# A planned two-layer graph network kernel: the planner's ranks, slack and stage orders take new values at set times

## The chip, the cores and the metric

The kernel runs on one core of a Trainium2 chip. The metric is device time in microseconds (us) of one execution of the whole program; several executions are made and their median is given. A profile is one more execution, with its own time.

In this text PE is the engine that multiplies matrices (with PEld, its weight loads), DVE the vector engine, ACT the engine for activation functions, POOL the general-purpose engine and SP the engine that issues most DMAs (transfers). PSUM is the memory that PE writes to; it has eight banks. Each engine works through its own queue of instructions in order.

## The reference

The input is a batch of 64 graphs with 256 nodes each, 256 features a node, and an integer adjacency matrix a graph. Two layers follow each other; all numbers are 32-bit floats.

```python
def _gat(h, adj, W, a, out_features):
    Wh = jnp.matmul(h, W)
    e = jax.nn.leaky_relu(jnp.matmul(Wh, a[:out_features]) + jnp.swapaxes(jnp.matmul(Wh, a[out_features:]), 1, 2), negative_slope=0.2)
    att = jax.nn.softmax(jnp.where(adj > 0, e, NEG), axis=1)
    return jnp.matmul(att, Wh)

# layer 0
h = _gat(_gat(x, adj, W1, a1, Fout), adj, W2, a2, W2.shape[1])
h = _layernorm(x + h, g_ln1, b_ln1)
x = _layernorm(h + jax.nn.relu(h @ w_ff1 + b_ff1) @ w_ff2 + b_ff2, g_ln2, b_ln2)      # 256 -> 1024 -> 256

# layer 1: 8 heads of 32, four value matrices Wv[r], one for each value of adj
attn = softmax(q @ k.T / sqrt(32))
out = sum over r of (attn * (adj == r)) @ (x @ Wv[r] + bv[r])
x = _ln(x + out @ Wo + bo, g1, beta1)
x = _ln(x + gelu(x @ W1 + b1) @ W2 + b2, g2, beta2)
```

## The kernel before

**Pairs and stages.** The 64 graphs are worked on as 32 pairs. A pair goes through four stages (`whole_way`): `gat_layers` (the two graph attentions of layer 0), `feed_forward` with relu, `attention` (layer 1) and `feed_forward` with gelu. Several pairs are under way at a time, each in another stage. The names "gat", "ff" and "attention" can each be held by one pair at a time.

**The matmuls.** The products of the first feed-forward layer and of q, k and v are made by the class `Blocks`: seven products of half-size blocks (steps p1 to p7, each 0.86 us in the plan) instead of eight, with the sums between them done by DVE (line 449, rank "blocks") and copies out of PSUM by ACT (line 757 in feed-forward, rank "copies"; line 763 applies the activation function, rank "act"). "a1" is product 1 of the first half of the work, "b3" product 3 of the second; `FIRST` and `QKV` are the orders in which these steps are taken, and "s0" and "s1" in `QKV` are the scores of the first two groups of heads. The second feed-forward layer (`by_seven`) has seven products of 64 matmuls, with DVE sums of the inputs (`combine`, line 831, rank "sums") and DVE additions of the results to the rows (line 828, rank "last"). Nearly all matmuls are issued by `by_strips` at line 122, four strips of 32 columns each. The scores (line 943) are multiplied in tiles of another shape, 32 rows. A group of scores takes four PSUM banks; ACT exponentiates them (line 952, rank "exp"), DVE masks them (956, "mask") and adds halves (960, "halves"), and `products` (lines 974 and 977) multiplies them by the values. `GROUPS` is the order of these groups of scores and products. `layernorm` uses ACT for squares (659), DVE to centre (668) and scale (671), and POOL for the root (664, 665); `means` (645, ACT) is the mean after `by_seven`. `transposed` turns rows on DVE (692, rank "turn") and sends them by SP through a scratch buffer back to SBUF as `yT`; attention copies that on ACT (883, rank "piece").

**The planner.** When the program is built, `run` simulates the engines with a clock each, and emits instructions in the order in which the simulation takes them. That order is final: `keep_order` chains each engine's instructions. Work for DVE, ACT, POOL and SP is handed in with `put`, with a duration, the events that it needs and a rank. When an engine is free, it takes of the pieces that are ready the one of the lowest rank (`RANK`), and of equal ranks the one that was ready first. PE is filled by Python generators, one a pair: each yields the events, the names and the banks that its next step needs, and `took` moves PE's clock by the step's duration. A step is sure if it was ready `SLACK` (0.3 us) ago; of the sure ones the one of the lowest `DEGREE` of its kind (first, gat, attention, fill, rows) is taken, and if none is sure the one that is ready first. A change of tile shape costs 0.1 us of plan time. `FLIGHT` (6) is the number of pairs that may be begun. All these are constants for the whole plan.

The chip follows the emitted order, with its real durations; where they differ from the plan's, an engine waits on semaphores.

```python
able = [n for at, n in times if at <= now]
...
sure = [n for at, n in times if at <= now - SLACK]
g = going[min(sure, key=lambda n: (going[n][0] is besides, degree(going[n]), n))
          if sure else min(times)[1]]
...
piece = waiting[engine].pop(min(able, key=lambda n: (waiting[engine][n]["rank"], waiting[engine][n]["first"]["ready"])))
```

Of the kernel before, what the change touches and what calls it, by code (L numbers as in the profile page):

```python
# [18 lines left out]
P = 128  # L19
# [9 lines left out]
SHAPES = ("rows",)  # L29
SLACK = 0.3  # L30
FLIGHT = 6
RANK = {"adj": 1, "second": 0.5, "blocks": -1, "exps": 1.5, "addends": 0.5, "weigh": 3, "ratios": -0.5, "squares": 0.5,
        "copies": -2, "act": -1, "last": -1, "sums": -0.5, "qk": 1, "v": 1.5, "exp": 3, "mask": 0, "halves": 0, "invert": 3,
# [9 lines left out]
def two_layers(ctx: ExitStack, tc: tile.TileContext, t: dict, out: bass.AP, flag: bass.AP):  # L43
# [70 lines left out]
    psum = ctx.enter_context(tc.tile_pool(name="psum", bufs=8, space=bass.MemoryType.PSUM))  # L114

    def bank():
        return psum.tile([P, 512], F32, name="ps")

# [37 lines left out]
    clock = dict(START)  # L156
    waiting = {engine: [] for engine in engines if engine != "tensor"}
    alone, filling, shaped = {}, [], [None]
    free = {name: [0.0] * n for name, n in (("bank", 8), ("a", HQ), ("m", HQ), ("h", HQ), ("yb", 1), ("yT", 2), ("yTa", 1),
# [80 lines left out]
    def run(besides, ways, together):  # L240
# [7 lines left out]
        def degree(g):  # L248
            kind = ("fill" if g[0] in filling else "first" if "ff" in (g[2] or ()) or alone.get("ff") is g[0] else
                    "attention" if "attention" in (g[2] or ()) or alone.get("attention") is g[0] else "gat")  # L250
            return DEGREE["after" if shaped[0] and shape(g) else shape(g) or kind]

        together += 1
        while True:
            while len(going) < together and (way := next(ways, None)) is not None:
                going.append([way, *next(way)])
# [21 lines left out]
            if engine == "tensor":  # L278
                sure = [n for at, n in times if at <= now - SLACK]
# [10 lines left out]
                if step is None:  # L290
                    together -= g[0] is besides
                    going.remove(g)
                else:
                    g[1:] = step
# [23 lines left out]
    def load(pair, at=None):  # L318
# [29 lines left out]
        def in_bytes(there):  # L348
            return put("vector", 1.35, largest, put("scalar", 1.2, small_adj, there, needs="adj", rank=RANK["adj"]), rank=RANK["adj"])
# [51 lines left out]
    class Second:  # L401


        def __init__(self, b, name, *events):
            self.b, self.name, self.there, self.read = b, name, [], []
            for n in range(3):
                self.there.append(put("vector", 0.34, lambda n=n: self.add(n), *events, rank=RANK["second"], needs=None if n else name))
                events = self.there[-1:]
            self.there.append(Event())
# [8 lines left out]
        def read_by_second(self, event):  # L418
            self.read.append(event)
            if len(self.read) == 2:  # L420
                put("vector", 0.34, lambda: self.add(3), self.there[2], *self.read, rank=RANK["second"], event=self.there[3])
# [7 lines left out]
    class Blocks:  # L429
# [5 lines left out]
        def __init__(self, second, first, begin, multiply, target, copy, corner, finished):  # L435
            self.second, self.first, self.begin, self.bank, self.u3, self.fifth = second, first, begin, {}, None, None
            self.multiply, self.target, self.copy, self.corner, self.finished = multiply, target, copy, corner, finished

        def product(self, n, to, a, first=False):
            if first:  # L440
                self.bank[to] = self.bank[to] if n == 5 else bank().rearrange("p (n c) -> p n c", n=2)
# [5 lines left out]
        def add(self, c, h, bank, *events, frees=()):  # L447
            def add():
                nc.vector.tensor_tensor(self.target(c, h), self.bank[bank], self.target(c, h), ALU.add)  # L449
            there = put("vector", 0.6, add, *events, rank=RANK["blocks"], frees=frees)  # L450
            self.finished(c, h, there)
            return there

        def p1(self):
            yield *self.first, 1
            self.begin()
            self.u1 = self.copy(0, 0, self.product(1, "x", 0, True))

        def p2(self):
            yield [], None, 1  # L460
            there = self.product(2, "z", 1, True)
            self.c11 = self.add(0, 0, "z", self.u1, there)
            self.second.read_by_second(there)

        def p5(self):
            yield [self.c11, self.second.there[0]], None, 0
# [3 lines left out]
        def p6(self):  # L470
            yield [self.u1, self.second.there[1]], None, 0
            self.u2 = self.copy(0, 1, self.product(6, "x", 3))

        def p7(self):
            yield [self.u2, self.second.there[2]], None, 0
            self.u3 = self.copy(1, 1, self.product(7, "x", 4))
            self.add_fifth()

        def add_fifth(self):
            if self.u3 and self.fifth:  # L480
                self.c22 = self.add(1, 1, "z", self.u3, self.fifth)

        def p4(self):
            yield [self.u3, self.second.there[3]], None, 0
            self.corner(self.bank["x"], self.product(4, "x", 6))

        def p3(self):
            yield [self.c22], None, 0
            self.add(0, 1, "z", self.u2, self.product(3, "z", 5), frees=["bank"])


    def addends(y, there, at, layer, pair):
# [20 lines left out]
        there = put("scalar", 0.6, exps, *there, rank=RANK["exps"], function="exp")  # L513
# [28 lines left out]
        there = put("vector", 0.2, turn, there, rank=RANK["addends"])  # L542
# [3 lines left out]
    def gat_weights(y, at, at_home, ratio, there, to, b):  # L546
# [20 lines left out]
        there = put("vector", 0.95, lambda: weigh(0), *there, rank=RANK["weigh"] + b / 2, needs="e")  # L567
        there = put("vector", 1.13, lambda: weigh(1), there, rank=RANK["weigh"] + b / 2, frees=["rows"] * b)
        return of, put_each("scalar", 0.4, [lambda j=j: scale(j) for j in range(2)], there, rank=RANK["ratios"])

    def gat_layers(pair, to, loads):
# [3 lines left out]
        def evacuated(to, k, wide, ps):  # L575
            return put("scalar", 0.3, lambda: nc.scalar.activation(to[:, k, :wide], ps[:, :wide], AF.Copy),
                       took(0.88), rank=RANK["evac"], frees=["bank"])
# [30 lines left out]
        for b in range(2):  # L608
# [9 lines left out]
            transposed(to["x"], layernorm(to["x"], ln[0], b, added, biased[0]), normal, b, pair, 0)  # L618
# [4 lines left out]
    def add_rows(y, p, b, *events):  # L623
# [12 lines left out]
        return of, put_each("vector", 0.44, [lambda j=j: add(j) for j in range(2)], *events, rank=RANK["rows"], frees=["bank"])  # L636

    def means(y, b, *events):
# [8 lines left out]
        return of, put_each("scalar", 0.54, [lambda j=j: mean(j) for j in range(2)], *events, rank=RANK["means"])  # L647

    def layernorm(r, gb, b, added, *events):
# [11 lines left out]
        def root():  # L661
# [3 lines left out]
            nc.gpsimd.tensor_tensor(rstd, rstd, mhalf[:, :2], ALU.pow)  # L665

# [6 lines left out]
        there = put_each("scalar", 0.54, [lambda j=j: square(j) for j in range(2)], there, rank=RANK["squares"])  # L673
        centred = put_each("vector", 0.4, [lambda j=j: centre(j) for j in range(2)], there, rank=RANK["centre"])
        there = put("gpsimd", 1.2, root, there, rank=0)
        return put_each("vector", 0.4, [lambda j=j: scale(j) for j in range(2)], there, centred, *events, rank=RANK["scale"])
# [5 lines left out]
    def transposed(y, ready, to, b, pair, stage):  # L682
# [23 lines left out]
        there = put("vector", 0.62, turn, ready, rank=RANK["turn"], needs="yb")  # L706
# [25 lines left out]
    def feed_forward(y, normal, w, func, relieved, gb, pair, stage):  # L732
# [11 lines left out]
        def slabs(t):  # L744
# [11 lines left out]
            def copy(c, h, event):  # L756
                return put("scalar", 0.5, lambda: nc.scalar.activation(target(c, h), blocks.bank["x"], AF.Copy), event, rank=RANK["copies"])  # L757

            def activate(c, h, event, of=None, frees=()):
                for n in range(2):  # L760
# [3 lines left out]
                        to, source, func, bias=b1[:, m:m + 1]), event, rank=RANK["act"] + h, function=kind,  # L764
# [4 lines left out]
            blocks = Blocks(second, first, begin, multiply, target, copy,  # L769
                            lambda of, event: activate(1, 0, event, of, ["bank"]), activate)  # L770
            return blocks
# [3 lines left out]
        for step in FIRST:  # L775
            yield from steps[step]()
        yield from (by_seven if stage in SEVEN else by_eight)(y, normal, f, evacuated, w2, w2_there, b)
        for g in range(2):
            normal[g] = layernorm(y, gb, g, normal["added"][g], *([biased[1]] if onwards else []))
# [5 lines left out]
    def by_eight(y, normal, f, evacuated, w2, w2_there, last):  # L785
# [3 lines left out]
        for g in range(2):  # L789
            for j in range(2):  # L790
                for part in (order[:half], order[half:]):
# [8 lines left out]
                    if g == j == 0 and part[0] == 0:  # L800
                        yield from last.p3()
# [3 lines left out]
    def by_seven(y, normal, f, evacuated, w2, w2_there, last):  # L805
# [14 lines left out]
        def product(n, to, side, first=False):  # L820
# [4 lines left out]
            return took(1.8)  # L825

        def add(to, of, us, *events, frees=()):
            return put("vector", us, lambda: nc.vector.tensor_tensor(to, of, to, ALU.add), *events, rank=RANK["last"], frees=frees)  # L828

        def combine(to, a, b, op, *events):  # L830
            return put("vector", 1.14, lambda: nc.vector.tensor_tensor(to, a, b, op), *events, rank=RANK["sums"])  # L831

        def two_halves():
            return bank().rearrange("p (j b d) -> p j b d", j=2, b=2)
# [6 lines left out]
        yield [w2_there, *done(0, 0)], None, 1  # L841
        left = two_halves()
# [4 lines left out]
        x = two_halves()[:, 0]  # L847
# [3 lines left out]
        yield from last.p3()  # L851
# [3 lines left out]
        v = two_halves()[:, 0]  # L855
# [6 lines left out]
        d24 = add(rows[:, :, :, :P], left, 0.6, read2, read4, frees=["bank"])  # L862
# [9 lines left out]
    def attention(y, normal, pair, all_adj):  # L872
# [13 lines left out]
        there = put("scalar", 0.52, lambda: in_one_piece(0), normal[0], rank=RANK["piece"], needs="yTa")  # L886
        there = put("scalar", 0.52, lambda: in_one_piece(1), there, normal[1], rank=RANK["piece"], frees=["yT"])
# [27 lines left out]
        def with_bias_qk(c, b, event, frees=()):  # L915
# [654 lines left out]
```

## Time and profile before

| what | value |
| --- | --- |
| median of 3 executions | 2944.82 us (2944.0 to 2946.82) |
| the profiled execution: its time | 2945.81 us |
| the profiled execution: its span, first to last instruction | 2944.0 us |
| PE busy / DVE busy / ACT busy | 2881.8 / 2618.9 / 1859.3 us |
| mean granted clock of PE | 0.992 |
| largest group on PE: the 128x128 matmuls of the second feed-forward layers | 14336 of 419.1 us busy and 14336 of 422.5 |
| largest group on DVE: the masks (L956) and the sums (L831) | 256 of 311.2 us busy and 256 of 310.4 |
| largest group on ACT: the exponentials (L952) | 512 of 269.8 us busy, 600 ns each |

The span is the time from the first to the last instruction in the profile; the time of an execution also has what lies around it. Busy time is the union of an engine's instructions. A view of stretches gives for each window its length, then busy time and number of instructions of PE, PEld, DVE, ACT and POOL, then the granted clock of PE (1.00 is full), the share of the DMA engines and GB/s. A line of waits reads: who waited, for what, how many us in all, how many times, the longest. A line of the timeline reads: start, us busy, engine, line, operation, tiles, shape, count and, in brackets, idle time before it and what ended that. "ps" is a PSUM bank, "ff" an intermediate of feed-forward.

### The profile page before, as it was taken

What the parts mean: (1) busy time and instruction counts of PE and PEld (TensorE: products, weight loads), DVE (VectorE), ACT (ScalarE), POOL (GpSimd) and SP (SyncE); (2) the same over time, 40 slices, a digit from 0 to 9 for tenths busy, and PEclk for the clock granted to TensorE, in tenths of its full rate; (3) what the DMA queues carried; (4) which work ended last, traced back from release to release, by engine and by line L of the source; (5) the groups of instructions that cost most, each with busy time, mean ns of one, the idle gap of its engine ahead of it and who ended that gap; (6) DMA issues with size and microseconds to landing.
All of it is one profiled execution on the core that took longest, in us unless ns stands there. A gap on an engine that the chain in (4) does not pass through costs nothing.

```text
span 2944.0 us, 147796 instructions
## 1 busy us (share of the span) xinstructions
PE 2881.8 (98%) x66066; PEld 2025.8 (69%) x66066; DVE 2618.9 (89%) x5873; ACT 1859.3 (63%) x5124; POOL 267.4 (9%) x518
## 2 busy tenths in 40 slices
PE   6999999999999999999999999999999999999998
PEld 4776766667767667767677667677666666676776
DVE  5899999889988889988889989899988898889886
ACT  3666666666665666665766665766665665666555
POOL 0010100010000100000101000100110100011001
PEclk7999999999999999999999999999999999999999
DMA  6222222222122221222221222221222221222100
GB/s 181 69 69 71 75 65 84 67 85 71 60 74 75 89 75 61 70 68 85 88 76 61 69 70 85 83 81 51 69 75 82 82 74 55 72 69 70 44 3 25
DMA packets 214179, 211.84 MB, mean 72 GB/s; under 512 B 22945, under 2 KB 173089, under 8 KB 213537
## 3 DMA queue, kind: packets, MB, share of 16 engines
q1 hardware_dynamic: 213120, 202.06, 21.5%
q8 instruction: 520, 8.52, 1.2%
q14 instruction: 123, 1.00, 0.1%
q10 hardware_dynamic: 416, 0.26, 0.0%
HBM read 137.51 MB, written 64.73 MB: 69 GB/s over the span
## 4 chain that ended last, share of the span: by engine, by line
PE 64%; DVE 27%; issue 3%; ACT 2%; DMA 2%; SPq 1%; POOL 0%; DVEq 0%; POOLq 0%; ACTq 0%
PE ps L122 56%; DVE ff L831 4%; PE ps L974 4%; DVE m L956 3%; PE ps L943 3%; DVE ff L449 3%; DVE x L671 2%; DVE x L668 2%; DVE h L960 2%; DVE x L828 2%; DVE yb L692 2%; PE ps L977 1%; DVE x L631 1%; DVE e L558 1%; DMA home<-yb 1%
## 5 line engine op out<-in xcount | busy, mean ns | idle before, releaser
L952 ACT ACTIVATE a<-ps 128x512 f32<-128x512 f32 x512 | 269.8, 600 | 297.0 <-PE ps L943 274.1
L122 PE MATMUL ps<-w_L_gnn_W,ff 128*32 128x128 f32 x14336 | 419.1, 273 | 16.3 <-DVE ff L831 10.7
L122 PEld LDWEIGHTS ps<-w_L_gnn_W,ff 128*32 128x32 f32 x14336 | 394.5, 110 | 44.1 <-DVE ff L831 18.3
L122 PE MATMUL ps<-w_L_gnn_w_ff,ff 128*32 128x128 f32 x14336 | 422.5, 273 | 1.0 <-DVE ff L449 0.5
L122 PEld LDWEIGHTS ps<-w_L_gnn_w_ff,ff 128*32 128x32 f32 x14336 | 389.6, 110 | 41.2 <-issue 16.6
L122 PE MATMUL ps<-yT,w_L_gnn_W1p 128*32 128x256 f32 x5120 | 313.9, 379 | 1.5 <-DVE qk L997 0.8
L122 PE MATMUL ps<-yT,w_L_gnn_w_ff1p 128*32 128x256 f32 x5120 | 312.8, 379 | 2.2 <-ACT ff L757 2.1
L831 DVE TENSOR_TENSOR ff<-ff 128x1024 f32<-128x1024 f32 x256 | 310.4, 1212 | 4.3 <-PE ps L122 3.6
L449 DVE TENSOR_TENSOR ff<-ps,ff 128x512 f32<-128x512 f32 x384 | 259.0, 679 | 61.3 <-ACT ff L757 42.7
L664 POOL TENSOR_SCALAR rstd<-squares 128x2 f32<-128x2 f32 x256 | 70.6, 276 | 2649.3 <-ACT unread L659 2647.3
L956 DVE TENSOR_TENSOR m<-a,adj 128x1024 f32<-128x1024 f32 x256 | 311.2, 1215 | 0.0
L659 ACT ACTIVATE unread<-x,less 128x256 f32<-128x256 f32 x512 | 259.1, 506 | 80.5 <-DVE less L634 48.6
L757 ACT ACTIVATE ff<-ps 128x512 f32<-128x512 f32 x384 | 225.3, 591 | 102.6 <-PE ps L122 100.6
L763 ACT ACTIVATE ff<-ff,c_L_gnn_b 128x256 f32<-128x256 f32 x384 | 174.7, 503 | 131.6 <-DVE ff L449 131.0
L122 PE MATMUL ps<-xw,e 128*32 128x258 f32 (+1 forms) x4096 | 246.1, 386 | 6.8 <-ACT xw L565 6.8
L122 PEld LDWEIGHTS ps<-yT,w_L_gnn_W1p 128*32 128x32 f32 x5120 | 165.7, 110 | 111.2 <-DVE qk L997 1.8
L122 PEld LDWEIGHTS ps<-yT,w_L_gnn_w_ff1p 128*32 128x32 f32 x5120 | 166.6, 110 | 107.5 <-ACT ff L757 3.6
L763 ACT ACTIVATE ff<-ff,c_L_gnn_b_ff 128x256 f32<-128x256 f32 x384 | 176.7, 502 | 75.9 <-DVE ff L449 75.6
L828 DVE TENSOR_TENSOR x<-ps,x 128x256 f32<-128x256 f32 (+1 forms) x384 | 192.7, 502 | 28.6 <-PE ps L122 26.4
L665 POOL TENSOR_TENSOR rstd<-rstd,mhalf 128x2 f32<-128x2 f32 x256 | 196.1, 766 | 21.3
L122 PEld LDWEIGHTS ps<-xw,e 128*32 128x32 f32 x4096 | 133.1, 112 | 90.7 <-ACT xw L565 9.0
L960 DVE TENSOR_TENSOR h<-a 128x512 f32<-128x512 f32 x256 | 174.7, 682 | 0.0
(132 smaller groups left out, 4969.9 us busy)
## 6 DMA issues: line engine op xcount, KB each, us to landing
home<-yb SPq DMA_DIRECT2D x182, 256.0 KB, 2.1
yT<-home SPq DMA_DIRECT2D x728, 64.0 KB, 2.1
rows<-row SPq DMA_DIRECT2D x60, 512.0 KB, 4.3
input<-in_xT SPq DMA_DIRECT2D x32, 512.0 KB, 4.0
x<-in_x SPq DMA_DIRECT2D x32, 512.0 KB, 3.9
out<-x SPq DMA_DIRECT2D x64, 256.0 KB, 3.3
input<-in_adjT SPq DMA_DIRECT2D x30, 512.0 KB, 4.1
v<-in_adjT SPq DMA_DIRECT2D x2, 512.0 KB, 7.3
```

The source lines that it names most:

```text
L122: nc.tensor.matmul(to[at:at + DH], lhsT=lhsT[:, at:at + DH], rhs=rhs, **flags)
L449: nc.vector.tensor_tensor(self.target(c, h), self.bank[bank], self.target(c, h), ALU.add)
L659: nc.scalar.activation(unread, rows[j], AF.Square, bias=of["less"][:, j:j + 1], accum_out=squares[:, j:j + 1])
L665: nc.gpsimd.tensor_tensor(rstd, rstd, mhalf[:, :2], ALU.pow)
L757: return put("scalar", 0.5, lambda: nc.scalar.activation(target(c, h), blocks.bank["x"], AF.Copy), event, rank=RANK["copies"])
L763: evacuated[h][m] = put("scalar", 0.4, lambda m=m, to=to, source=source: nc.scalar.activation(to, source, func, bias=b1[:, m:m + 1]), even ...
L828: return put("vector", us, lambda: nc.vector.tensor_tensor(to, of, to, ALU.add), *events, rank=RANK["last"], frees=frees)
L831: return put("vector", 1.14, lambda: nc.vector.tensor_tensor(to, a, b, op), *events, rank=RANK["sums"])
L952: nc.scalar.activation(a[n][q][:, k], ps[2 * q + k], AF.Exp)
L956: nc.vector.tensor_tensor(m[n][q], a[n][q], adj, ALU.mult)
L960: nc.vector.tensor_tensor(h[n][q], a[n][q][:, :, :N], a[n][q][:, :, N:], ALU.add)
L974: nc.tensor.matmul(po[o * DH:(o + 1) * DH, :N], lhsT=v[:, b, jc, at:at + DH], rhs=e[o // 2][:, o % 2, jc * N:(jc + 1) * N], start=r == jc ...
```

## The change

A table `CHANGES` gives, for times of PE's clock in the plan 90 us apart, new values of ranks, of degrees and of the settings "slack", "flight", "first", "qkv" and "groups". `run` puts them in force once PE's planned clock has passed their time. A stage that is under way keeps the order that it began with.

```diff
+NORMED = ()
+CHANGES = (
+    (27.0, ("all", "slack", 0.2), ("rank", "means", 0)),
+    (117.0, ("rank", "means", 1)),
+    (207.0, ("all", "qkv", ("a1", "b1", "b2", "a2", "a6", "a5", "b6", "a7", "a4", "b5", "b7", "a3", "b4", "s0", "b3", "s1")),
+     ("rank", "adj", 1), ("rank", "normalise", 2), ("rank", "exp", -1)),
+    (297.0, ("degree", "fill", 1), ("all", "groups", (([0], []), ([1], []), ([], [2]), ([], [3]), ([2], []), ([3], []))),
+     ("degree", "first", -1), ("all", "slack", 0.3)),
+    (387.0, ("degree", "fill", 2.5), ("all", "slack", 0.8), ("rank", "mask", 1.5), ("rank", "turn", 2),
+     ("all", "first", ("a1", "b1", "a6", "a2", "b2", "b6", "a5", "a7", "b7", "a4", "b5", "b4", "a3"))),
+    (477.0, ("all", "slack", 0.1)),
+    (657.0, ("rank", "qk", 2), ("rank", "adj", 0), ("rank", "act", 0.5), ("rank", "last", 0.5)),
+    (1197.0, ("rank", "invert", 1.5), ("rank", "adj", -1), ("rank", "exps", -0.5),
+     ("all", "first", ("a1", "b1", "a2", "a6", "b2", "b6", "a5", "a7", "b7", "a4", "b5", "b4", "a3")),
+     ("rank", "normalise", 0), ("degree", "rows", 2)),
+    (1287.0, ("rank", "turn", 1)),
+    (1377.0, ("all", "groups", (([0], []), ([1], []), ([], [2]), ([], [3]), ([2], []), ([3], []))), ("rank", "divide", 1.5),
+     ("rank", "copies", -2), ("all", "flight", 5)),
+    (1467.0, ("all", "first", ("a1", "b1", "a2", "a6", "b2", "b6", "a5", "a7", "b7", "b5", "a4", "b4", "a3")),
+     ("rank", "addends", 0.5)),
+    (1557.0, ("rank", "copies", 1), ("rank", "qk", -2)),
+    (1827.0, ("rank", "copies", -2)),
+    (1917.0, ("rank", "v", 1)),
+    (2007.0, ("rank", "rows", 1.5), ("rank", "squares", -0.5), ("rank", "copies", 0)),
+    (2367.0, ("rank", "last", 1), ("rank", "adj", -0.5), ("degree", "attention", 0)),
+    (2547.0, ("rank", "divide", 1), ("rank", "mask", 3)),
+    (2637.0, ("degree", "first", 2.5)),
+    (2727.0, ("rank", "last", 3), ("rank", "second", 0.5)),
+    (2817.0, ("all", "first", ("a1", "b1", "a2", "a6", "b2", "b6", "a5", "a7", "b7", "b5", "a4", "b4", "a3")),
+     ("rank", "second", -0.5), ("rank", "rows", -2)),
+)
+KEPT = 0
+SEEDS = {"ff": (), "qk": (), "v": ()}
...
         while True:
-            while len(going) < together and (way := next(ways, None)) is not None:
+            while changes and clock["tensor"] >= changes[0][0]:
+                _, of, name, value = changes.pop(0)
+                of[name] = value
+            while len(going) < settings["flight"] + any(g[0] is besides for g in going) and (way := next(ways, None)) is not None:
                 going.append([way, *next(way)])
...
-                sure = [n for at, n in times if at <= now - SLACK]
+                sure = [n for at, n in times if at <= now - settings["slack"]]
...
-        there = put("vector", 0.95, lambda: weigh(0), *there, rank=RANK["weigh"] + b / 2, needs="e")
+        there = put("vector", 0.93, lambda: weigh(0), *there, rank=rank_of["weigh"] + b / 2, needs="e")
...
-            return put("scalar", 0.3, lambda: nc.scalar.activation(to[:, k, :wide], ps[:, :wide], AF.Copy),
-                       took(0.88), rank=RANK["evac"], frees=["bank"])
+            return put("scalar", 0.27, lambda: nc.scalar.activation(to[:, k, :wide], ps[:, :wide], AF.Copy),
+                       took(0.88), rank=rank_of["evac"], frees=["bank"])
...
-        return of, put_each("scalar", 0.54, [lambda j=j: mean(j) for j in range(2)], *events, rank=RANK["means"])
+        return of, put_each("scalar", 0.45, [lambda j=j: mean(j) for j in range(2)], *events, rank=rank_of["means"])
...
-            return took(1.8)
+            return took(1.745)
...
-        for step in FIRST:
+        order = settings["first"]
+        for step in order:
             yield from steps[step]()
```

Everywhere else `RANK[...]` becomes `rank_of[...]`, a copy of the table that `CHANGES` writes to. Beside this, the diff restructures `Blocks`, `by_seven` and `layernorm` so that banks can be set aside (`KEPT`), sums can be started in PSUM (`SEEDS`, rank "seeds") and a layernorm can be scaled on ACT (`NORMED`, rank "normalise"). With `KEPT` at 0 and the other two empty, as here, these branches do nothing, but for one new tile `nothing` of 128x1 that DVE sets to zero at the start:

```diff
+    nothing = const.tile([P, 1], F32, name="nothing")
+    nc.vector.memset(nothing, 0.0)
+    kept = [kept_bank() for _ in range(KEPT)]
```

## The prediction, made before the result was known

> **What bounds the kernel now.** First the page's head, for the engine nearest to the span, then the chain that ended last, for what the end hangs on.
>
> ```profile
> span 2944.0 us, 147796 instructions
> PE 2881.8 (98%) x66066; PEld 2025.8 (69%) x66066; DVE 2618.9 (89%) x5873; ACT 1859.3 (63%) x5124; POOL 267.4 (9%) x518
> ...
> PE 64%; DVE 27%; issue 3%; ACT 2%; DMA 2%; SPq 1%; POOL 0%; DVEq 0%; POOLq 0%; ACTq 0%
> ```
>
> PE (the matmuls) leaves 62 us of the span idle. DVE holds 27% of the chain because the chain follows whatever released a step, and DVE is nearly as full; it doesn't mean that PE stood still for it. So I cut the span into stretches of 90 us, about one pair each, and read PE's busy time, the first number after the comma.
>
> ```profile
> 27.00:117.00 90.00, 79.99 (x1460) 55.37 (x1456) 63.86 (x176) 45.71 (x129) 6.88 (x12) 0.83 0.32 91
> ...
> 387.00:477.00 90.00, 87.75 (x2044) 61.45 (x2040) 82.66 (x188) 56.73 (x159) 9.05 (x18) 1.00 0.24 76
> 477.00:567.00 90.00, 87.05 (x1992) 60.91 (x1986) 77.36 (x170) 56.54 (x153) 6.72 (x12) 0.98 0.23 73
> ...
> 657.00:747.00 90.00, 89.73 (x2076) 62.85 (x2072) 82.34 (x185) 58.43 (x163) 8.35 (x17) 1.00 0.23 73
> ...
> 2187.00:2277.00 90.00, 87.95 (x1996) 60.65 (x1992) 81.34 (x177) 59.43 (x163) 8.88 (x16) 1.00 0.23 76
> 2277.00:2367.00 90.00, 87.85 (x2032) 61.13 (x2024) 82.28 (x191) 57.13 (x159) 7.87 (x16) 1.00 0.24 77
> 2367.00:2457.00 90.00, 87.36 (x1992) 60.19 (x1988) 78.83 (x178) 59.55 (x160) 9.10 (x16) 1.00 0.22 69
> ```
>
> The middle (657 to 2007) is periodic: the chain's longest pieces start at 889.55, 978.33, 1067.11, ... us, 88.78 us apart, and PE idles 0.27 us in 90. No plan can take more than that idle there without changing the matmuls, of which this change changes none. The loose time is in four places. Start: 10.0 us idle in 27:117. From 117 on, the 31 stretches idle 28.1 us together (2790.0 less 2841.89 - 79.99 = 2761.9 busy); at the steady rate they would idle 31 x 0.28 = 8.7, so **19.4 us are irregular**, mostly between 207 and 657 and between 2007 and 2637. Third, a stall of 0.20 us that most pairs of the middle repeat, some 17 times, 3.4 us. Fourth, the edges: 6.55 us before the first matmul (a weight's DMA) and 11 us after the last one.
>
> PE's own waits say who is late:
>
> ```profile
> PE ps L122 <- DVE ff L831: 11.1, 26, 2.1
> PE ps L122 <- ACT xw L565: 6.8, 2, 4.4
> ...
> PE ps L122 <- DVE ff L449: 5.0, 5, 1.9
> ...
> PE ps L122 <- ACT ff L757: 3.9, 6, 1.0
> PE ps L122 <- ACT ff L763: 3.6, 2, 2.5
> ```
>
> L831 is `combine`, the sums that the second feed-forward layer needs; L449 adds up a block of the first. Both are DVE work whose place in DVE's queue is set by a rank (`sums`, `blocks`) against all other ranks. L565 belongs to the start.
>
> **The change part by part.** *What is off.* KEPT is 0 and SEEDS and NORMED are empty, so the new branches of `Blocks`, `by_seven` and `layernorm` emit what was emitted before; `normalise` and `seeds` rank nothing. New is one memset of 128x1, at most 0.14 us (L503's row of a 128x1 result), under the 6.55 us that PE waits for its first weight: 0. Both forms of the count of pairs in flight give the same. Flight 5 from 1377 on: `x` has four buffers, and only one pair is in each of `gat`, `ff` and `attention`, so a sixth pair could only wait: 0. The entries of 1377 for `groups` and of 2817 for `first` set the value that stands: 0.
>
> *Durations.* They are the planner's, and move no instruction by themselves. `by_seven`'s product goes from 1.8 to 1.745: PE's timeline has 64 such matmuls at 1291.48 and the next block at 1293.23, so 1.75. The old value put PE 14 x 0.05 = 0.7 us a pair later than it is, so a `combine` looked ready when it wasn't; that fits the 0.20 us that repeats. I take **-1.5** of the 3.4 (bounds 0 and -3.4).
>
> *Ranks and degrees, for the irregular stalls.* Of PE's waits, those on DVE (11.1 and 5.0 above, and 1.7 on L828 and 0.8 on L997 further down the same list: 18.6, less the repeated 3.4) are 15.2 us, and those are a matter of order: DVE is idle 7.6 us of 90 in the steady stretch, and ranks of `mask`, `turn`, `rows`, `last` moved back let sums go first. Ranks on ACT matter less: `exp` goes from last to near the front at 207, but before its instructions (L952) ACT idles 297 us in all, 274 of them waiting for PE's scores, so they go at once already. Stalls by way of ACT are less in reach. The longest, 2.52 us before 538.41, has ACT holding at a copy of `yT` for its DMA (1.92 us idle) with the activation PE needs behind it; the lags that the planner gives to DMAs stay as they are. I take two thirds of 15.2: **-10** (bounds 0, and all 19.4). A matmul that isn't late then meets the next limit, DVE's queue at 82 of 90, so not all can go.
>
> *The clock.* After that stall the granted clock is half for 3.4 us (0.98 in that stretch), which costs 1.7. Gone with it, or elsewhere again: **-1** (0 to -1.7). The Trainium skill (TensorE: Matmul & The Clock Gate, "Why this matters for your kernels") says that the clock holds if no gap is over about 3 us. Here 2.52 us were enough, while 2.05 us before 2232.43 were not. By the rule this term would be 0.
>
> *Stage orders.* `first`, `qkv` and `groups` permute the same matmuls. What they can save is a change of tile shape: the scores (32 rows) stand alone at every place of the timeline that I read.
>
> ```profile
> 1282.76 1.26 PE L122 MATMUL ps<-yT,w_L_gnn_w_ff1p 128*32 128x256 f32 x20
> 1283.95 1.15 PE L943 MATMUL ps<-qk 32*128 32x256 f32 x16
> 1285.03 3.70 PE L122 MATMUL ps<-w_L_gnn_w_ff,ff 128*32 128x128 f32 x128
> ```
>
> From 1283.95 to 1285.03 are 1.08 us for 16 matmuls that elsewhere take 0.86, and 0.11 lie ahead of them: 0.33 us for each lone group, four a pair. The new `groups` puts the third and fourth next to each other. But each needs four of eight banks, which ACT frees at 0.60 us an exponential, and other steps hold some: an actual meeting is rare. **-1** (bounds 0, and two meetings a pair in 29 pairs, 19). Moving b3 between s0 and s1 only fills the wait for banks: 0.
>
> *Slack.* From 477 to the end a step counts as sure when it was ready 0.1 us ago by the plan, not 0.3. What is queued behind a wrong guess is all of PE, in order. The trace's error of one step isn't shown, but the repeated 0.20 us is what one wrong guess costs. I take 0.13 us a pair over 27.4 pairs: **+3.5** (bounds 0, and four such stalls a pair, 0.8 x 27.4 = 22).
>
> *Start and end.* At 27 only `means` and the slack move; the 4.62 us before the weights for v and the 3.0 before the first transposes wait for loads and for a first chain that nothing overlaps: 0 (4 either way). At the end only DVE's order changes, under PE: 0.
>
> **Sum:** -1.5 - 10 - 1 - 1 + 3.5 = -10. The profiled execution took 2945.81 (2944.0 span, 1.8 around it), 1.0 over the median 2944.82; the median less 10 is **2935 us**.
>
> **Rivals.**
> (1) *All stalls go.* Every irregular and repeated stall and the clock's loss: -24.5, 2920; with half of the scores meeting, 2911. For it: the periodic middle shows that PE can run with 0.27 idle. Against: yT's DMAs, and 32 pairs with one rank table each need luck at the joints.
> (2) *Reshuffled.* The stalls come at other places with the same sum: 2945, 5 either way. For it: the plan after 27 us is a new one everywhere, the middle's included, which has nothing to gain. Against: the stalls come in two clusters, which looks like orders that didn't suit them.
> (3) *Too little slack: slower.* From 477 on PE goes ahead of sums and activations that are 0.1 to 0.3 us late. Four stalls of 0.2 a pair cost 22, less the 13.5 otherwise won: 2953 or more. It decides, past 0.2%, from (13.5 + 5.9) / 27.4 = 0.7 us a pair, that is when PE idles 1.0 in 90 in the middle. For it: the steady period already has such a stall in most pairs. Against: the durations are nearer to the rows now, and a wait under 0.2 is often absorbed.
>
> **How the numbers follow.** Forecast (2927 to 2938.9) 0.50; all go (below 2927) 0.14; reshuffled 0.19; slower 0.17. About 0.2%, 5.9 us, is what a measurement of this kernel tells from no change. Faster by more: 0.50 + 0.14 = 0.64; within: 0.19; slower: 0.17. From the rivals' ends I leave out the part under 2918 (0.06) and over 2953 (0.12): range **2918 to 2953**; the forecast alone 2927 to 2939.
>
> **What would show it.** PE idle from 117 on falls from 28 to about 18 us: right; the two clusters gone but the middle over 0.6 idle in 90: the slack's term was too small. The wait on L831 down from 11.1 to under 6 confirms ranks and durations. Fewer than 128 separate L943 groups: the scores meet. The granted clock at 1.00 in all stretches after 117: the clock's term. Wrong altogether if the middle's period leaves 88.8 us by over 0.3 either way, which is 4 us or more by itself, or if the stretch 27:117 moves by over 4.

## The result, and the profile after

The changed kernel takes **2929.66 us** (median of 6, 2921.04 to 2935.39) against 2946.19 for the kernel before (median of 6, 2944.0 to 2950.51): ratio **0.9938**, 95% interval 0.992 to 0.9956. That is faster, by 16.5 us between the medians. The profiled execution took 2928.64 us, with a span of 2926.9, 17.1 shorter than before's 2944.0.

First the page's head and the chain of the changed kernel.

```profile
span 2926.9 us, 147784 instructions
PE 2874.6 (98%) x66066; PEld 2062.1 (70%) x66066; DVE 2629.6 (90%) x5874; ACT 1847.4 (63%) x5120; POOL 274.1 (9%) x518
...
PE 4%; DVE 2%; ACT 1%; issue 0%; DMA 0%; POOL 0%; DVEq 0%; SPq 0%; POOLq 0%; ACTq 0%
```

The number of matmuls is the same. Of the 17.1 us, PE's idle time gives 9.9 (62.2 to 52.3) and its busy time 7.2. As the matmuls are the same, that is the clock (some 5 us, half of the 10 us by which its times at half clock are shorter) and the small joints between blocks. The chain is of no use here: its shares add up to 7%, because it could be followed back only to a DMA at 2693 us. So the stretches must carry the reading. In each line the first number after the comma is PE's busy time.

```profile
27.00:117.00 90.00, 85.64 (x1644) 57.99 (x1640) 71.42 (x198) 53.70 (x148) 6.66 (x12) 0.91 0.38 110
...
387.00:477.00 90.00, 89.98 (x1956) 60.66 (x1948) 83.03 (x190) 61.51 (x171) 8.10 (x16) 1.00 0.24 73
477.00:567.00 90.00, 90.00 (x2164) 64.92 (x2164) 81.26 (x194) 61.03 (x166) 11.34 (x20) 1.00 0.27 84
...
837.00:927.00 90.00, 86.77 (x1988) 59.81 (x1980) 78.59 (x177) 56.96 (x155) 8.41 (x16) 0.98 0.23 70
927.00:1017.00 90.00, 87.55 (x2020) 61.01 (x2016) 80.49 (x182) 57.05 (x159) 8.70 (x16) 1.00 0.23 69
...
1197.00:1287.00 90.00, 87.23 (x1980) 60.42 (x1976) 76.83 (x179) 54.90 (x155) 8.80 (x16) 0.98 0.25 78
...
2187.00:2277.00 90.00, 90.00 (x2086) 63.78 (x2082) 83.91 (x191) 58.47 (x166) 7.92 (x16) 1.00 0.24 73
2277.00:2367.00 90.00, 89.95 (x2069) 69.96 (x2064) 82.57 (x185) 57.92 (x162) 7.72 (x16) 1.00 0.23 73
2367.00:2457.00 90.00, 90.00 (x2076) 79.04 (x2072) 82.17 (x181) 60.86 (x168) 10.57 (x20) 1.00 0.23 73
```

Three things are to be seen. The start idles 4.4 us instead of 10.0. Both clusters of stalls are gone: PE idles 0.8 us between 207 and 657 (8.2 before) and 0.2 us between 2007 and 2637 (11.5 before). And the middle, which had been nearly clean, is not: between 657 and 2007 it idles 15.3 us (6.4 before), most of it from 837 to 1287. Two of the same stretches in the kernel before, the first of them one of the two in its middle that idle over 1 us:

```profile
837.00:927.00 90.00, 88.53 (x2052) 61.91 (x2046) 81.05 (x183) 57.38 (x160) 8.06 (x17) 1.00 0.24 73
...
1197.00:1287.00 90.00, 89.72 (x2100) 63.35 (x2096) 82.28 (x188) 58.47 (x163) 7.82 (x16) 1.00 0.23 73
```

Since both kernels do the same matmuls, I weigh each matmul of the trace by its columns, add them up, and compare the times at which the two have done the same amount of work. A negative number: the changed kernel is ahead.

| stretch (time in the kernel before) | changed in it, us | ahead at its end, us |
| --- | --- | --- |
| 0 to 71 | -10.0 | -10.0 |
| 71 to 205 | +3.4 | -6.6 |
| 205 to 679 | -11.2 | -17.8 |
| 679 to 886 | -1.9 | -19.7 |
| 886 to 1402 | +12.6 | -7.1 |
| 1402 to 2020 | +1.0 | -6.1 |
| 2020 to 2649 | -13.6 | -19.7 |
| 2649 to 2918 | +2.7 | -17.0 |

PE's waits name the engines:

```profile
PE ps L166 <- ACT xw L650: 10.6, 5, 3.2
...
PE ps L166 <- ACT xw L639: 5.8, 2, 5.4
...
PE ps L166 <- ACT ff L845: 2.2, 3, 1.4
...
PE ps L166 <- DVE ff L920: 1.3, 3, 0.6
```

L920 is `combine` (L831 before): its 11.1 us are down to 1.3. L650 is `evacuated`, ACT's copy of the graph attention's products out of PSUM (L576 before); no wait of PE on it stood in the list of before, and it is the largest now. The half-clock time at the start is 24 us (20.1 to 30.4, 40.6 to 47.5, 54.3 to 61.1) against 37.5 before; half of the difference, 6.7, is most of what the start gains beside 3.7 less idle.

Why L650 is late stands in the timeline around the longest such stall:

```profile
882.13 0.63 ACT L973 ACTIVATE yTa<-yT 128x512 f32<-128x512 f32 x1 [2.93 <-DMA yT<-home]
882.66 0.40 ACT L719 ACTIVATE unread<-x 128x256 f32<-128x256 f32 x1
...
886.63 0.51 ACT L733 ACTIVATE unread<-x,less 128x256 f32<-128x256 f32 x1
...
887.14 0.64 ACT L650 ACTIVATE xw<-ps 128x258 f32<-128x258 f32 x2
...
887.56 3.38 PE L166 MATMUL ps<-yT,w_L_gnn_w_ff1p 128*32 128x256 f32 x32 [3.23 <-ACT xw L650]
```

ACT stands 2.93 us at the copy of `yT` into `yTa`, which waits for its DMA; eight activations stand between that and the two copies that free PE's banks, and PE has idled 3.23 us. SP's own waits show that the DMAs are in a new situation: before a gather of `yT`, SP waited for the store's landing 93.4 us in 55 waits before, and 313.9 us in 136 waits now. The line of the kernel before comes first.

```profile
SPq L703 <- DMA home<-yb: 93.4, 55, 4.3
```

```profile
SPq L791 <- DMA home<-yb: 313.9, 136, 5.5
```

### The profile page after: what moved, and what is told of

It reads as the page before. It is cut to its first block, busy times and chain, and to the rows that moved or that the text cites. A ratio compares the mean times of both kernels' runs of the same rounds, so it can differ in the third digit from the quotient of the medians.

```text
span 2926.9 us, 147784 instructions
## 1 busy us (share of the span) xinstructions
PE 2874.6 (98%) x66066; PEld 2062.1 (70%) x66066; DVE 2629.6 (90%) x5874; ACT 1847.4 (63%) x5120; POOL 274.1 (9%) x518
## 5 line engine op out<-in xcount | busy, mean ns | idle before, releaser
L166 PEld LDWEIGHTS ps<-w_L_gnn_w_ff,ff 128*32 128x32 f32 x14336 | 397.3, 110 | 36.3 <-issue 13.0
L166 PE MATMUL ps<-yT,w_L_gnn_w_ff1p 128*32 128x256 f32 x5120 | 321.4, 382 | 10.8 <-ACT xw L650 10.6
L920 DVE TENSOR_TENSOR ff<-ff 128x1024 f32<-128x1024 f32 x256 | 311.2, 1215 | 16.0 <-PE ps L166 12.6
L738 POOL TENSOR_SCALAR rstd<-squares 128x2 f32<-128x2 f32 x256 | 78.2, 306 | 2625.1 <-ACT unread L733 2622.5
L166 PEld LDWEIGHTS ps<-yT,w_L_gnn_w_ff1p 128*32 128x32 f32 x5120 | 172.6, 110 | 113.6 <-ACT xw L650 13.5
L166 PEld LDWEIGHTS ps<-yT,w_L_gnn_W1p 128*32 128x32 f32 x5120 | 171.9, 110 | 100.1 <-ACT ff L845 5.7
L917 DVE TENSOR_TENSOR x<-ps,x 128x256 f32<-128x256 f32 (+1 forms) x384 | 191.8, 504 | 33.8 <-PE ps L166 30.4
L1007 ACT ACTIVATE qk<-ps,bqk 128x256 f32<-128x256 f32 x256 | 109.3, 468 | 118.3 <-PE ps L166 117.3
```

Source lines behind the costliest of these rows:

```text
L166: nc.tensor.matmul(to[at:at + DH], lhsT=lhsT[:, at:at + DH], rhs=rhs, **flags)
L738: nc.gpsimd.tensor_scalar(rstd, squares, 1.0 / D, EPS, ALU.mult, ALU.add)
L1007: nc.scalar.activation(target_qk(c, b)[:, n], of[:, n], AF.Identity, bias=bqk[:, n, c:c + 1])
```

## The experiments

The planner has a clock of its own, so each plan states how long PE idles in it. That gives a theory with numbers. **Theory A**: the chip follows the plan; what the table does is take idle time out of the plan, as one piece fitted to the four durations. The main rival, **B**: small differences between plan and chip swamp this, and the new time is a draw among plans of the same kind. After the profile came **theory F** for the new stalls: ACT held by the DMA, with PE's copies queued behind.

### Parts of the change alone

Four kernels: the durations alone, the table with the old durations, the table's first two entries, and its entries up to 477.

```diff
-CHANGES = (
-    (27.0, ...
+CHANGES = ()
```

> The changed kernel with an empty table: the four new durations alone. Theory A (the chip follows the planned order, and PE idles about where the plan has it idle): the plan's PE clock has 140 us of idle here, against 57 in the kernel before and 19 in the changed one, so the time is about 2946 + 83 = 3029 us, between 3000 and 3050. Rival B (small differences between plan and chip swamp the plan's idle; any plan of this kind gives about the same): 2946, 15 either way. Rival C (better durations are a gain by themselves, as the prediction's term of -1.5 has it): 2935 to 2945.

```diff
-        there = put("vector", 0.93, lambda: weigh(0), ...
+        there = put("vector", 0.95, lambda: weigh(0), ...
...
-            return took(1.745)
+            return took(1.8)
```

> The changed kernel with its table but the old four durations. Theory A: the plan idles 103 us, 46 more than before, so about 2992 us, between 2975 and 3015. Rival B: 2946, 15 either way. Rival D (the table's orders are good whatever the durations are): 2925 to 2940, near the changed kernel.

```diff
     (117.0, ("rank", "means", 1)),
-    (207.0, ("all", "qkv", ...
...
+)
```

> New durations and only the table's entries at 27 and 117. Up to 297 the planned orders are those of the changed kernel. Theory A: the start up to 60 us on the chip keeps the gain of 10 us that the changed kernel has there, and after that the plan idles 3.07 us in every 90, so PE idles about 2 to 4 us in each stretch of the middle; the plan has 101 us of idle, so about 2946 + 43 = 2989 us, 2970 to 3010. Rival B: 2946, 15 either way.

```diff
     (477.0, ("all", "slack", 0.1)),
-    (657.0, ("rank", "qk", 2), ...
...
+)
```

> New durations and the table's entries up to 477, held from there on. Up to 657 the planned orders are those of the changed kernel. Theory A: the gain up to 657 stays (16 to 18 us ahead of the kernel before); after that the plan idles 1.0 us in 90, about the 0.93 of the kernel before, and 18 us near 2850 which it doesn't have; the plan's idle is 66 us, 9 over that of before, so about 2955 us, 2940 to 2975. Rival E (the entries after 657 do nothing, since the plan of before is periodic there and has nothing to gain): 2925 to 2935, like the changed kernel.

Then two that leave out one kind of entry: all for the slack, and all for stage orders. The second of them leaves out more than its expectation says: with the order "first" went the two entries for the degree of the kind "first", at 297 and at 2637.

```diff
-    (27.0, ("all", "slack", 0.2), ("rank", "means", 0)),
+    (27.0, ("rank", "means", 0)),
...
-    (477.0, ("all", "slack", 0.1)),
```

> The changed kernel without the table's entries for slack: 0.3 all along. Theory A, now with a scale: in the six kernels measured so far the time is the plan's last PE time, at the new duration of a product, plus 33 to 74 us, 57 on average. Here the plan ends PE at 2979, so 3036 us, between 3012 and 3053. Rival I (the slack's term of the prediction: less slack costs 3.5 us, so 0.3 all along is a little better than the table): 2922 to 2932.

```diff
-    (207.0, ("all", "qkv", ...), ("rank", "adj", 1), ...
+    (207.0, ("rank", "adj", 1), ...
...
-     ("degree", "first", -1), ("all", "slack", 0.3)),
+     ("all", "slack", 0.3)),
...
-    (2637.0, ("degree", "first", 2.5)),
```

> The changed kernel without the table's entries for stage orders (first, qkv, groups): the orders of before all along, with the table's ranks, degrees and slack. Theory A: the plan ends PE at 2991, so 3048 us, between 3024 and 3065. Rival J (the orders' term of the prediction: they are worth 1 us): 2927 to 2934.

In the table the plan's last PE time is given at 1.745 us a product; for the two plans with 1.8 that takes 448 x 0.055 = 24.6 us off, time that the chip doesn't take, since a product there lasts 1.75 us.

| kernel | PE idle in the plan | plan's last PE time | measured median | ratio to before (95%) |
| --- | --- | --- | --- | --- |
| before | 57 | 2900 | 2946.19 | |
| changed | 19 | 2862 | 2929.66 | 0.9938 (0.992 to 0.9956) |
| durations alone | 140 | 2983 | 3016.16 | 1.0243 (1.0226 to 1.0261) |
| table, old durations | 103 | 2946 | 3019.24 | 1.0258 (1.0238 to 1.0278) |
| entries at 27 and 117 | 101 | 2944 | 3001.22 | 1.0189 (1.0171 to 1.0207) |
| entries up to 477 | 66 | 2909 | 2971.22 | 1.0089 (1.0067 to 1.0112) |
| without slack | 136 | 2979 | 3052.19 | 1.0364 (1.034 to 1.0388) |
| without stage orders and the degree of "first" | 148 | 2991 | 3043.16 | 1.0329 (1.0312 to 1.0346) |

**Each of the six kernels with only some of the change is slower than the kernel before**, by 0.9 to 3.6%, and all six are as slow as theory A has it, to within 27 us (the one with the old durations is 4 us above A's range). B, C, D, E and I fall. J isn't tested: the kernel without stage orders lacks the two degrees as well, so no run says what the orders are worth by themselves. The time is the plan's last PE time plus 33 to 74 us. So the plan is a good guide for large differences, and a poor one for the last 20 us: of the 38 us that the change takes out of the plan (57 to 19), 17 arrived.

Where the plan idles says the same. In the plan of the kernel before, PE idles 10 us between 207 and 657 and 13 us between 2007 and 2637, in that of the changed kernel 3 and 0: the two clusters stood in the old plan, and the new one has taken them out. But from 657 to 2007 the plan goes from 14 us of idle to 0.04, and the chip from 6.4 to 15.3. That is where the gain of the plan didn't arrive.

The durations alone show how a part can be a loss. A stretch of their middle, and PE's waits:

```profile
1557.00:1647.00 90.00, 87.87 (x2030) 61.46 (x2024) 79.56 (x182) 57.29 (x159) 8.01 (x16) 1.00 0.21 70
```

```profile
PE ps L137 <- ACT a L1017: 28.6, 21, 1.4
PE ps L137 <- DVE ff L891: 23.8, 34, 1.4
PE ps L137 <- ACT xw L621: 16.2, 21, 0.8
```

The plan settles in another period there, with 4.2 us idle in 90 in the plan and 2 to 3 on the chip (2.1 in the stretch shown, 2.9 in most). New durations shorten nothing by themselves; they only make the planner take other orders, and the single rank table that had suited the old durations doesn't suit the new ones. (Nor are all four nearer to the trace: two accumulating copies of L645, planned at 0.54 before and 0.45 now, follow each other by 0.54 us from start to start in the trace of before.) The entries up to 477 give the other half of the picture. On the chip that kernel is 14 us ahead of the kernel before when that has come to 575 us (the changed kernel: 17), and then loses all of it: it is level at 1917, and ends 25 us behind, as the plan loses 18 us in the stretch from 2817. Against rival E: the later entries gain nothing over the kernel before until 2020 us, but without them the gain of the first 600 us doesn't last.

### Who holds ACT

The emission of one instruction can be changed while the plan stays as it is. Here the copy of `yT` goes to POOL; PE, DVE, SP and the rest of ACT keep their order.

```diff
-            nc.scalar.activation(yT[:, b].rearrange(...), normal["yT"][:, b].rearrange(...), AF.Copy)
+            nc.gpsimd.tensor_copy(yT[:, b].rearrange(...), normal["yT"][:, b].rearrange(...))
```

> The changed kernel with one thing moved: the copy of yT into yTa, which waits for a DMA, is done by POOL and not by ACT. The planned order of PE, DVE, SP and of the rest of ACT is the same, instruction for instruction. Theory F (the new stalls of the changed kernel between 840 and 1310 us come from ACT standing at this copy for a late DMA, with the copies out of PSUM that PE needs queued behind it): PE's waits on L650 fall from 10.6 us to under 4, and the time to about 2922 us, 2914 to 2927. Rival G (ACT is late because its own work is longer than planned, 0.54 us for a mean planned at 0.45): the waits stay over 8 us, the time 2926 to 2934. Rival H (POOL, for which no row shows a copy of this size, is too slow, and q, k and v come late instead): new waits of PE on POOL, over 2936 us.

> The same move in the kernel before. ACT waits 67.3 us for yT's DMA there, but of PE's waits only the 2.52 us before 538.41 and parts of the 3.9 on L757 lie behind it. Theory F: 2 to 5 us less, about 2943. Rival G: no change, 2944 to 2948. Rival H: as for the changed kernel, slower, by 6 us or more.

In the changed kernel: 2924.39 us, ratio to before 0.9926 (0.9913 to 0.994). PE's waits on L650 fall from 10.6 to 1.9 us, and the stretch from 886 to 1402 that had given back 12.6 us gives back 1.2.

```profile
PE ps L166 <- ACT xw L639: 5.2, 4, 3.6
...
PE ps L166 <- ACT xw L650: 1.9, 2, 1.1
```

In the kernel before: 2941.1 us, ratio 0.9982 (0.9973 to 0.9991), 5 us less, the upper end of what F expected. F holds; G falls, since the waits are gone while ACT's accumulations are as long as they were; H falls as a whole, though the copy takes 718 ns on POOL in the mean against 627 on ACT before. But of the 11.4 us that the move won from 886 to 1402, only 5 were left in the time, as it lost elsewhere. So there are three more runs: the changed kernel again, the move again, and the move only where the plan stands between 780 and 1290 us.

```diff
+            if 780.0 <= clock["tensor"] < 1290.0:
+                nc.gpsimd.tensor_copy(yT[:, b].rearrange(...), normal["yT"][:, b].rearrange(...))
+                return
             nc.scalar.activation(yT[:, b].rearrange(...), normal["yT"][:, b].rearrange(...), AF.Copy)
```

> The changed kernel once more, on the chip of the next two. If its stalls between 840 and 1310 us belong to the order and not to one execution, they are at the same matmuls in this profile: PE's waits on L650 8 us or more, ahead of the kernel before by about 20 us at 870 and by 6 to 9 at 1300. Time 2924 to 2935.

> The copies on POOL once more, beside the changed kernel on one chip. Theory F: 3 to 8 us under the changed kernel. If the first difference was one of chips or executions: within 2 us of it.

> The changed kernel with the copies moved to POOL only where the plan stands between 780 and 1290 us, 11 instructions; elsewhere ACT makes them as before. The order on PE is the same. Theory F says that this takes what the move wins (10 to 12 us of progress between 870 and 1310 in the first such profile) and leaves out the 8 to 10 that it lost elsewhere: 8 to 10 us under the changed kernel, about 2920, and waits on L650 under 3 us. If the losses elsewhere were not due to the move but are scatter of an execution: no better than the move everywhere, 2922 to 2927.

All on one chip: the changed kernel 2928.16 us, ratio 0.9948 (0.993 to 0.9966); the move everywhere 2923.82, 0.9924 (0.9903 to 0.9946); the move there only **2919.81, 0.9913 (0.9893 to 0.9932)**, 8.4 us under the changed kernel by the medians. It is the fastest of all, as expected. Its interval just touches that of the changed kernel, but each of its 5 executions (2916.11 to 2924.12) lies under each of the changed kernel's 7 (2924.41 to 2936.69). It moves 12 copies, not the 11 that its expectation counts: POOL has 530 instructions for 518, ACT 5108 for 5120. The move everywhere is 4.3 us under the changed kernel, as F has it, but their executions overlap. What it loses elsewhere repeats: both of its profiles show a new wait of 2.11 us for `combine`, at 182 and at 184 us, with half clock behind it, and at 575 us they are 12 and 10 us ahead of the kernel before, where the three profiles with ACT's copies there are 15 to 17 ahead. With the move there only, no wait of PE on L650 is over 1 us any more:

```profile
PE ps L166 <- DMA a<-in_L_gnn_W1T: 7.1, 1, 7.1
PE ps L166 <- ACT xw L639: 3.4, 2, 2.8
...
PE ps L166 <- ACT ff L845: 3.1, 4, 1.3
```

The second profile of the changed kernel missed what was expected of it: its waits on L650 are 5.1 us, not 8 or more, and at 1300 us it is 14 us ahead, not 6 to 9.

```profile
PE ps L166 <- ACT xw L650: 5.1, 4, 2.4
PE ps L166 <- ACT xw L639: 5.0, 3, 3.7
```

At the matmul that waited 3.23 us in the first profile it waits 0.17, at another 2.16 where the first waits 0.07, and at one it waits 2.40 where the first waits 1.80. It gives back 3.8 us between 886 and 1402 instead of 12.6, and idles 9.9 us between 657 and 2007 instead of 15.3. So the kind of the trouble belongs to the order, and its size to the execution: the DMA comes when it comes, and the plan has no time to spare for it. Whether the times scatter more for it isn't shown: the changed kernel's lie 14 us apart in its first 6 runs and those of the kernel before 6.5, but beside the last three runs those of the kernel before lie 17 us apart, in 12.

## Why the prediction was right, and where it wasn't

The total was right: 2935 forecast, 2929.66 measured, in the range and faster. That is in part luck. Two of its own signs of "wrong altogether" fired all the same: the start moved by 5.6 us of idle (bound 4), and the middle's pairs got 0.9 us longer (12.8 us between 679 and 1917, 14 pairs; bound 0.3). They have opposite signs. The sum held because errors cancelled. A third sign fired as well, the one for too small a slack term: with both clusters gone, the middle idles 1.0 us in 90 (0.7 in the second profile; bound 0.6). PE's idle time from 117 on fell from 28.1 to 21.8 us (19.4 in the second profile), where 18 was forecast. Step by step:

- **Irregular stalls, -10 of 19.4**: right in place, too small. Both clusters went, 8.2 + 11.5 to 0.8 + 0.2, which is 18.7, the steady rate of 3.4 in these 12 stretches included. "Not all can go" failed: with DVE at 82 to 84 of 90 the waits for `combine` are 1.3 us in 3. That ranks and degrees did it isn't shown: no kernel has them alone, and with them but without the slack's entries it takes 3052 us.
- **The repeated stall, -1.5 of 3.4**: all of it went (L920 down to 1.3 us in 3 waits). But the argument, that a truer duration takes it away, is refuted for the new durations by themselves: in that kernel PE waits 23.8 us for `combine`.
- **Slack, +3.5**: right in sign, and the step whose mechanism failed. The new stalls are 12.5 us of idle from 117 on (2.4 up to 207, 8.9 in the middle, 1.2 at the end; 3.5 in the middle in the second profile), and their largest part, 10.6 us of waits on L650, comes from DMAs that land later than planned, ahead of PE's copies in ACT's queue: with the copy of `yT` on POOL 1.9 us of them are left. A slack of 0.3 us wouldn't have covered the four long ones, of 1.8 to 3.2 us. That mechanism stood in the prediction, in the lines on the stall before 538.41, as a reason why stalls would stay; that a new plan could bring more of them was left out. What the slack of 0.1 costs by itself is not separated: without the slack's entries the whole plan changes, and the kernel takes 3052 us.
- **Start, 0 (4 either way)**: failed, -10.0. The two entries at 27 and 117 keep this gain (8.0 ahead at 71 us in that kernel). Of the two it is the slack of 0.2 that moves the order: the kernel without the slack's entries keeps `means` at 27, and its PE has the order of before up to 99 us. Some of the gain isn't due to order: three kernels with the start's order of before (the durations alone, the one without slack, and the kernel before with the copies on POOL) were 5.2, 3.3 and 2.3 ahead there as well, with 27 to 31 us at half clock against 37.5, and eight with the new order 8.0 to 10.8. So the order is worth some 6 or 7 us.
- **Clock, -1**: the stall at 538 and its half clock went; two new ones came, at 887 and 1252. +1.7 instead.
- **Stage orders, -1**: there are still 128 lone groups of scores, so 0 as a saving. Without them and the degree of "first" the kernel takes 3043 us, so one of the two at least is needed for the fit.
- Reshuffled (0.19) describes the middle; "all go" the two clusters. "Too little slack" had the right place for the loss; the cause of its largest part was another.

Still open: what makes the DMAs late. Of the stores whose gather starts within 6 us, 49 in the changed kernel are issued right behind another gather (within 1.2 us of the start of its last DMA), 11 in the kernel before. For 22 of these 49 their own gather starts more than 3.4 us after the store, against 33 of the other 110. The plan counts 64 KB for the four DMAs of a gather, which move 64 KB each. And among these stores one during which a 16 KB packet of the instruction queue is under way takes 3.5 us (median of 107) from its issue to the next gather, 2.08 without one (median of 53); a longer one meets more of them, so this shows no cause. No run separated the two.

## What to carry to other kernels

When a program is laid out ahead by a plan, judge its constants and its orders together: new durations made this kernel 2.4% slower until the orders were fitted to them, and each of the six kernels with only some of the change was a loss. An engine that the plan leaves no idle time is where differences between plan and chip come out, so look for what waits on a DMA in a queue that the bound engine also depends on, and move that to an engine that has time: that gave another 8 us, by 12 instructions, where moving all 64 gave about half of it by the medians. And a sum that comes out right is no proof of its terms; read them one by one against the stretches.

## What the runs showed of the hardware

A gap on PE of the same length does not always cost clock. In the kernel with the entries at 27 and 117 alone, PE idles 2.40 to 2.43 us once a pair from 708 to 2644, 21 times; 12 of them are followed by 3.4 us at half clock, 9 are not. One of each, seen by the 64 matmuls behind the gap:

```profile
707.92 3.50 PE L139 MATMUL ps<-w_L_gnn_W,ff 128*32 128x128 f32 x64 [2.43 <-DVE ff L893]
...
800.50 1.96 PE L139 MATMUL ps<-w_L_gnn_W,ff 128*32 128x128 f32 x64 [2.43 <-DVE ff L893]
```

The shortest gap after which it happened, past the start, is 2.04 us, and the longest one without is 3.25 us, both in the kernel without stage orders (before 2441 and before 2798 us). What decides is where the gap lies. In each of the 13 traces the granted clock changes only at times that are multiples of 3.413 us apart (to 0.005 us). These traces have 116 gaps of 1.5 us or more after the first 80 us. All 55 that put 2.04 us or more into one such step of 3.413 us are followed by half clock; of the 61 that put at most 1.93 us into any step, 58 are not (of the other three, two lie in a step already at half clock, and one, 2.97 us before 2540 in the kernel without slack, stays open). One half-clock step, at 2701 us in the second profile of the changed kernel, follows gaps of 1.3 us in all and isn't explained by this. The 12 gaps above put 2.21 to 2.43 us into one step, the 9 others 1.24 to 1.86. That is also why, in the kernel before, 2.52 us cost clock and 2.05 us did not: they put 2.26 and 1.26 us into one step.

The Trainium skill (TensorE: Matmul & The Clock Gate, "What's actually happening") describes a window of about 3.4 us that runs freely, and the steps of these traces fit it. Its advice ("Why this matters for your kernels") to have no gaps over about 3 us is too generous by these runs: even 2.04 us can cost clock.
